# A planned graph-attention layer: scan sums reckoned later behind their loads, and new planner constants

## The chip, the core and the metric

The kernel runs on one core of a Trainium2 chip. The metric is the device time of one execution in microseconds (us). Five engines work side by side, each through a list of its own, in order: PE (matrix products; its weight loads are shown as PEld), DVE, ACT, POOL, and SP, which here only issues DMA transfers. An engine that waits at one instruction holds up all that stands behind it in its list.

## What is computed

One layer of a graph network: a layer norm and a ReLU of x (384 nodes, 1024 features), masked attention with 16 heads of 64, whose queries, keys and values each go through two linear layers, an output layer, and the residual. The mask comes from 6528 edges: an edge that is listed puts a positive weight in its cell, all other cells are minus infinity.

```python
h = relu(layernorm(x))
q = h @ wq.T + bq;  k = h @ wk.T + bk;  v = h @ wv.T + bv          # 1024 x 1024 each
q2 = heads(q @ wiq.T + biq);  k2 = heads(k @ wik.T + bik);  v2 = heads(v @ wiv.T + biv)
mask = full(-inf);  mask[src, dst] = softplus(edge_type_weights)[edge_type - 1]
scores = einsum('hnd,hmd->hnm', q2, k2) / 8 + mask
out = x + (softmax(scores) applied to v2, heads side by side) @ wo.T + bo
```

## The kernel before

**Products.** Each operand is kept as a high and a low plane, so that each product is three matmuls (`mm3`, L450 to L452: high by high, high by low, low by high). A weight matrix is cut in 8 chunks of 128 rows. The chunks run in the order v, q, iv, k (32 chunks), then iq and ik in turn (16), then o (8). For each chunk SP loads 512 KB into one of four raw buffers (`load`, L99), ACT makes the high plane (`split_hi`, L124 or L128), DVE the low plane (`split_lo`, L135 or L137), and PE multiplies. Results stay in PSUM banks: three of kind g, four of kind s, one of kind a; a product waits until its bank has been emptied. What empties a bank is `k_f` (L574, then L579 and L582 make the planes of k), `v2_hi` and `v2_lo` (L639, L643), `qk_hi` and `qk_lo` (L696, L702) and the like.

**Scans.** Scales for the planes of iv, k, iq, ik and o need sums over the weights before their products are reached. So 40 further loads, eight for each of these matrices, go through three buffers of a tile `scan` (`scan_load`, L144), and ACT sums each one (`scan_sum`, L149). A scan buffer is free again when its sum is done. PE adds the sums over rows (`bound_sums` L532, `row_sums` L537), and DVE turns them into scales (`g_scale` L553 to L561, `common_scale` L564 to L566). The high planes of the iq chunks wait for the scale of gq, those of ik for that of gk.

**Mask.** DVE finds double edges (L295, 51 steps), POOL scatters the weights into tables in DRAM (L306, 51 steps), and loads them back (`mask_load`, L314, three loads). DVE takes them over (`mask_select`, L318) and scales them (L569).

**Attention and output.** For each pair of heads p there are three row blocks. PE makes scores of two heads (`do_S`, L711) in two s banks, DVE adds the mask and takes the row minimum (`do_ttr`, L719), which empties the bank, ACT takes the exponential (L723), DVE the reciprocal (L726, L730). The weights are then made two planes, on one of two routes chosen by the table `pool`: on POOL (L733, ACT L738, POOL L744) or on DVE (ACT L740, DVE L746). SP transposes them by DMA (L751), PE multiplies with v2 (`do_av`, L760), ACT and DVE make two planes (L764, L767). The output is seven tiles (a block of 128 rows by 512 columns each; the last block's second half is cut in two of 256), each over the eight o chunks (`omm`, a call of `mm3` per chunk). PE goes through tiles and chunks in an order set by the planner, and starts while the last score steps still run. Four output tiles stand in s banks and three in g banks; the first use of a g bank for a tile waits for `qk_lo` of the last chunks, that of an s bank for `do_ttr` of the last scores. `finish` (L788) adds the residual and the tiles go out.

**The planner.** None of this order is written by hand. Each step is a task with its engine, an assumed duration and its dependencies. First a list of PE tasks is made: `at` holds a place for each (constants `pre`, `rate`, `ds`, `da`, `avlag`, `sp`, and `last` for the ends of the output tiles). Due times run backwards from it (`needed`), with shifts for some kinds (`due`). Then a greedy loop takes, again and again, the task that can start first by its reckoning, and among equals the one due first, and writes its instructions. The start is the latest of: the engine is free (`act0`, `dve0`, `pool0` at the beginning), each dependency has ended plus a margin, a buffer is free. The margin behind a task of SP is `late`; behind others `wait`, and for PE `slack`. `gate` holds SP back from issuing far ahead, `mll`, `selat` and `selby` set when the mask is reckoned to be there. So a constant moves no instruction's work; it moves places in the five lists.

Of the kernel before, what the change touches and what calls it, by code (L numbers as in the profile page):

```python
# [24 lines left out]

P = dict(
    pre=11.98,
    rate=2.66,
    avlag=7,
    slack=0.6,  # L30
    act0=6.72,
    dve0=4.77,
    pool0=8.64,
    pb=6,
    lead=3,
    first=[7],
    gate=3.2,
    mll=3.72,
    ds=[0.0, 0.0, 0.0, 0.0, 0.0, 0.0, 0.0, 0.47, 0.47, 0.47, 0.47, 1.09, 0.47, 1.58, 0.47, 0.47, 0.47, 1.04, 0.62,
        0.47, 0.23, 0.47, 0.47, 1.14],  # L40
    da=[1.19, 0.16, 1.23, 1.19, 1.19, -0.39, -0.39, -0.39],
    pool=[0, 1, 0, 1, 0, 1, 0, 1, 0, 1, 0, 1, 0, 1, 0, 1, 0, 1, 0, 1, 0, 1, 0, 1, 0, 0, 0, 1, 0, 1, 0, 1, 0, 1, 0,
        1, 0, 0, 0, 1, 0, 1, 0, 0, 0, 0, 0, 1],
    last=[5, 1, 2, 0, 3, 6, 4],
    sp=dict(row=5.6, bv=41.0, biv=55.0, turn=75.6, kb=88.0, v2t=111.14, gq=118.19, gk=126.86, ob=149.12),
    due=dict(v2l=-0.13, ss=0.11, gkd=-2.65, lo=1.37),
    wait=0.08,
    late=0.27,
    selat=3.85,
    selby=1.62,  # L50
)


# [1 line left out]
def gnn_kernel(ctx: ExitStack, tc: tile.TileContext, x, edges, erows, etw, wq, wk, wv, wiq, wik, wiv, wo,  # L55
# [14 lines left out]
    ACT, DVE, POOL, SP = nc.scalar, nc.vector, nc.gpsimd, nc.sync  # L70
# [595 lines left out]
    end = {("lo", 0): 0.0, ("lo", 1): 5.3, ("hi", 2): 3.1, ("hi", 1): 2.1, ("load", 4): 6.8, "keys": 7.2}  # L666
# [282 lines left out]
    for p in range(8):  # L949
# [7 lines left out]
        for j in range(3 * p, 3 * p + 3):  # L957
# [10 lines left out]
            for o in range(2):  # L968
                pool = (j, o) in ON_POOL
# [68 lines left out]
    due = {}  # L1038

    def needed(n):  # L1040
        if n not in due:
            eng, dur, _, _, lag = tasks[n]
            due[n] = 0.0
            far = n[0] == "sc"
            d = min([needed(u) - (4.6 if far and u != ("sc", n[1] + 1) else 0 if tasks[u][0] == eng else lag)
                     for u in users[n]], default=now) - dur
            k = "elo" if n[0] == "lo" and len(n) == 3 else n[0] if isinstance(n, tuple) else n
            due[n] = min(d, at.get(n, d)) + P["due"].get(k, 0.0)
        return due[n]
# [4 lines left out]
    def port(n, eng):  # L1054

        return eng == "POOL" and n[0] != "sc" or eng == "DVE" and n[0] in ("lo", "ms", "sel", "vlo", "Qlo", "kl", "det")
# [5 lines left out]
    while left:  # L1062
        best = None
        for n, (eng, dur, _, deps, lag) in left.items():
            if not all(d in end for d in deps):
                continue
            start = max([free[eng], free["port"] if port(n, eng) else 0.0])
            for d in deps:
                e = tasks.get(d, ("", 0, 0, 0, 0.0))
                start = max(start, end[d] + (0 if e[0] == eng else e[4] + (P["slack"] if eng == "PE" else P["late"] if e[0] == "SP" else P["wait"])))  # L1070
            if eng == "SP" and 0 < dur and n[0] != "turn":
                start = max(start, free["DMA"] - P["gate"])
            if n[0] == "sel":
                start = max(start, TB + P["selat"] + n[1] * P["selby"])
            ok = True
            for i, tag in enumerate(alloc[n]):
                w = len(ring[tag]) + alloc[n][:i].count(tag) - RING[tag]
                for f in ring[tag][w] if w >= 0 else []:
                    if f in end:
                        start = max(start, end[f] + (0 if tasks[f][0] == eng else tasks[f][4]))  # L1080
                    else:
                        ok = False
            if ok:
                rank = (start, -1.0 if n in FIRST else at[n] if eng == "PE" else needed(n))
                if best is None or rank < best[0]:
                    best = rank, n
        if best is None:
            raise ValueError(str([(n, [d for d in left[n][3] if d not in end], alloc[n]) for n in list(left)[:12]]))
        (start, _), n = best
        eng, dur, fn, _, lag = left.pop(n)  # L1090
        end[n] = free[eng] = start + dur
        if port(n, eng):
            free["port"] = end[n]
        if eng == "SP" and 0 < dur and n[0] != "turn":

            free["SP"] = start + 0.48
            end[n] = free["DMA"] = max(free["DMA"], start + 1.1) + dur
        if n[0] == "sc":
            end["sd", n[1]] = start + 5.6
        for i, tag in enumerate(alloc[n]):  # L1100
            ring[tag].append([frees[n][i]] if len(frees[n]) > i else [])
        fn()
# [39 lines left out]
```

## Time and profile before

| what | value |
|---|---|
| three runs | 275.53, 272.44, 274.82 us; median 274.82 |
| the profiled execution | 274.47 us |
| its span | 272.8 us, so 1.67 us around it |
| granted clock of PE | 0.999 |
| DMA | 72.44 MB, mean 266 GB/s |

The profile is of one execution. Busy time is counted per engine; a timeline row has the start in us from the span's start, the duration, and in brackets how long the engine stood idle before it and what ended that. Matmuls are pipelined, so a row's duration is longer than the distance from one start to the next; where rows are merged, "x4" gives their number. A row of the page's groups has the count, the busy time, the mean in ns, and the idle time before. Tile names are the program's, without buffer numbers: `whl` the weight planes, `raw` the loaded chunk, `scan` the scan buffer, `g`, `s`, `a` the banks (g also names some tiles in SBUF), `vhl` the planes of v2, `ma` the mask.

### The profile page before, as it was taken

To read this page: it belongs to the slowest core of one execution; us is meant where nothing else is said; L and a number is where in the kernel's file an instruction comes from. 1 tells how busy PE (TensorE), PEld (TensorE's weight loads), DVE (VectorE), ACT (ScalarE), POOL (GpSimd) and SP (SyncE) were. 2 spreads that over 40 slices of the span, in tenths; PEclk is the share of its full clock that TensorE was granted. 3 is DMA by queue.
4 is the path that set the end of the run, shared out by engine and by line. 5 is a ranking of instruction groups with operands and counts; after the bars stand their busy time and mean duration, and the time that the engine had idled before them with its cause. 6 is when DMAs were issued, how large, how long until landed. Compare 5 with 4: busy or idle time off the path is not lost. (4 is left out here: it accounts for less than half of the span.)

```text
span 272.8 us, 5010 instructions
## 1 busy us (share of the span) xinstructions
PE 264.7 (97%) x1636; PEld 188.3 (69%) x1636; DVE 215.4 (79%) x537; ACT 207.4 (76%) x394; POOL 134.7 (49%) x142
## 2 busy tenths in 40 slices
PE   7899999999999999999999999999999999999994
PEld 6899999999984444899996555555555554444552
DVE  3775578999995675658697999999899899989033
ACT  3886769879897997586978859998989898794100
POOL 5764685545475655466610005556771464335900
PEclk9999999999999999999999999999999999999999
DMA  6899998896999998989899974799999979956415
GB/s 236 267 307 416 369 406 321 221 412 248 353 340 367 382 407 285 320 286 322 268 345 404 356 274 154 118 198 203 231 202 160 248 153 171 324 114 117 87 46 187
DMA packets 58922, 72.44 MB, mean 266 GB/s; under 512 B 42640, under 2 KB 43280, under 8 KB 58896
## 3 DMA queue, kind: packets, MB, share of 16 engines
q1 hardware_dynamic: 56688, 70.26, 83.9%
q0 software_dynamic: 2064, 1.80, 2.3%
q8 instruction: 13, 0.21, 0.3%
q14 instruction: 13, 0.11, 0.1%
q10 hardware_dynamic: 144, 0.07, 0.1%
HBM read 59.27 MB, written 3.39 MB: 230 GB/s over the span
## 5 line engine op out<-in xcount | busy, mean ns | idle before, releaser
L452 PE MATMUL g<-g,whl 128*128 128x384 f32 (+1 forms) x304 | 100.7, 331 | 0.8 <-DVE whl L135 0.5
L450 PE MATMUL g<-g,whl 128*128 128x384 f32 (+1 forms) x304 | 101.3, 333 | 0.0
L451 PE MATMUL g<-g,whl 128*128 128x384 f32 (+1 forms) x304 | 100.6, 331 | 0.0
L306 POOL DMA_INDIRECT tab<-edge x51 | 58.9, 1154 | 40.6 <-DMA tab<-edge 27.2
L149 ACT ACTIVATE scan<-scan 128x1024 f32<-128x1024 f32 x40 | 42.1, 1052 | 16.0 <-DMA scan<-in_wik_dram 5.4
L733 POOL TENSOR_TENSOR e<-e,st 128x384 f32<-128x384 f32 x20 | 22.9, 1146 | 52.7 <-DVE st L726 28.4
L137 DVE TENSOR_TENSOR whl<-raw,whl 128x1024 fp32r<-128x1024 f32 x22 | 27.1, 1230 | 19.2 <-ACT whl L128 12.7
L452 PEld LDWEIGHTS g<-g,whl 128*128 128x128 f32 x176 | 33.0, 188 | 0.6 <-issue 0.6
L450 PEld LDWEIGHTS g<-g,whl 128*128 128x128 f32 x176 | 33.1, 188 | 0.3
L451 PEld LDWEIGHTS g<-g,whl 128*128 128x128 f32 x176 | 33.1, 188 | 0.0
L723 ACT ACTIVATE e<-e,st 128x384 f32<-128x384 f32 x48 | 28.9, 603 | 3.0 <-DVE st L719 3.0
L744 POOL TENSOR_TENSOR pp<-e,pp 128x384 f16<-128x384 f32 x20 | 22.1, 1110 | 15.2 <-ACT pp L738 15.1
L719 DVE CUSTOM_DVE_ANT_0 e<-s,ma,cols 128x384 f32<-128x384 f32 x48 | 27.3, 607 | 0.0
L128 ACT ACTIVATE whl<-raw 128x1024 fp32r<-128x1024 f32 x23 | 24.1, 1048 | 4.1 <-POOL edge L253 2.0
L135 DVE SCALAR_TENSOR_TENSOR whl<-raw,small,whl 128x1024 f16<-128x1024 f32 x16 | 21.0, 1321 | 4.7 <-ACT whl L124 4.7
L450 PE MATMUL s<-whl,g 128*128 128x512 f16 (+2 forms) x65 | 23.6, 363 | 0.5 <-DVE st L719 0.5
L451 PE MATMUL s<-whl,g 128*128 128x512 f16 (+2 forms) x65 | 23.6, 363 | 0.0
L452 PE MATMUL s<-whl,g 128*128 128x512 f16 (+2 forms) x65 | 23.5, 363 | 0.0
L124 ACT ACTIVATE whl<-raw,small 128x1024 f16<-128x1024 f32 x16 | 18.1, 1141 | 5.6 <-DMA raw<-in_wo_dram 4.4
L450 PEld LDWEIGHTS <-whl 128*128 128x128 f16 x128 | 12.5, 98 | 12.1 <-issue 4.9
L135 DVE SCALAR_TENSOR_TENSOR whl<-raw,cols,whl 128x1024 f16<-128x1024 f32 x16 | 20.6, 1294 | 0.0
L746 DVE SCALAR_TENSOR_TENSOR pp<-e,st,pp 128x384 f16<-128x384 f32 x28 | 20.0, 741 | 0.6 <-ACT pp L740 0.5
(184 smaller groups left out, 456.3 us busy)
## 6 DMA issues: line engine op xcount, KB each, us to landing
raw<-in_wv_dram SPq DMA_DIRECT2D x8, 512.0 KB
scan<-in_wiv_dram SPq DMA_DIRECT2D x8, 512.0 KB
raw<-in_wq_dram SPq DMA_DIRECT2D x8, 512.0 KB
scan<-in_wk_dram SPq DMA_DIRECT2D x8, 512.0 KB
raw<-in_wiv_dram SPq DMA_DIRECT2D x8, 512.0 KB
scan<-in_wiq_dram SPq DMA_DIRECT2D x8, 512.0 KB
raw<-in_wk_dram SPq DMA_DIRECT2D x8, 512.0 KB
scan<-in_wik_dram SPq DMA_DIRECT2D x8, 512.0 KB
```

The source lines that it names most:

```text
L128: nc.scalar.activation(hi, raw[w], AF.Copy)
L135: nc.vector.scalar_tensor_tensor(lo, raw[w], sc, hi, op0=OP.mult, op1=OP.subtract)
L137: (eng or nc.vector).tensor_tensor(lo, raw[w], hi.bitcast(F32), OP.subtract)
L149: ACT.activation(x, x, AF.Abs if n in ("iv", "o") else AF.Square, accum_out=l1[:, j, m:m + 1])
L306: nc.gpsimd.indirect_dma_start(out=tabs[c // RNG], out_offset=bass.IndirectOffsetOnAxis(ap=idx[:, c:c + 1], axis=0), in_=val[:, c:c + 1], ...
L450: nc.tensor.matmul(ps, lhi, rhi, start=first, stop=False)
L451: nc.tensor.matmul(ps, lhi, rlo, start=False, stop=False)
L452: nc.tensor.matmul(ps, llo, rhi, start=False, stop=last)
L719: DVE.tensor_tensor_reduce(es[j][o], sps[j][o][:, :N], ma[:, j % 3, :], nscale, 3.0e38, OP.add, OP.min, sts[j][:, o:o + 1])
L723: ACT.activation(es[j][o], es[j][o], AF.Exp, bias=sts[j][:, o:o + 1], scale=-1.0, accum_out=sts[j][:, 2 + o:3 + o])
L733: POOL.tensor_tensor(es[j][o], es[j][o], sts[j][:, 4 + o:5 + o].to_broadcast([128, N]), OP.mult)
L744: POOL.tensor_tensor(pls[j, o][:, 1, :], es[j][o], pls[j, o][:, 0, :], OP.subtract)
```

## The change

There is one new constant, `dl`. In the planner's loop the margin behind a task of SP becomes `late + dl` if the waiting task is a scan sum (`ss`), so these sums are reckoned ready 0.568 us later than anything else that waits for a load. `late` itself goes from 0.27 to 0.336. Other constants are set anew, and with them the lists of all engines come out in another order. The work itself is nearly the same: the table `pool` loses one entry, so that one half of one score step (step 16, second head) goes by DVE and ACT and no longer by POOL. `last` sets another order of the output tiles' last chunks, and with it which tile comes last and is cut in two pieces.

```diff
@@ -25,29 +25,30 @@
-    rate=2.66,
+    rate=2.666,
-    act0=6.72,
-    dve0=4.77,
-    pool0=8.64,
+    act0=6.868,
+    dve0=5.838,
+    pool0=8.736,
-    gate=3.2,
-    mll=3.72,
+    gate=3.239,
+    mll=3.154,
...
-    da=[1.19, 0.16, 1.23, 1.19, 1.19, -0.39, -0.39, -0.39],
+    da=[1.19, 0.16, 1.23, 1.48, -0.3, -0.37, -0.37, -0.37],
...
-    last=[5, 1, 2, 0, 3, 6, 4],
-    sp=dict(row=5.6, bv=41.0, biv=55.0, turn=75.6, kb=88.0, v2t=111.14, gq=118.19, gk=126.86, ob=149.12),
-    due=dict(v2l=-0.13, ss=0.11, gkd=-2.65, lo=1.37),
+    last=[5, 0, 2, 6, 3, 4, 1],
+    sp=dict(row=5.6, bv=41.0, biv=55.55, turn=75.6, kb=88.0, v2t=111.14, gq=118.19, gk=126.86, ob=147.73),
+    due=dict(v2l=1.03, ss=0.11, gkd=-2.65, lo=1.37),
     wait=0.08,
-    late=0.27,
-    selat=3.85,
-    selby=1.62,
+    late=0.336,
+    dl=0.568,
+    selat=3.916,
+    selby=1.857,
...
@@ -1067,7 +1068,7 @@
-                start = max(start, end[d] + (0 if e[0] == eng else e[4] + (P["slack"] if eng == "PE" else P["late"] if e[0] == "SP" else P["wait"])))
+                start = max(start, end[d] + (0 if e[0] == eng else e[4] + (P["slack"] if eng == "PE" else P["late"] + (P["dl"] if n[0] == "ss" else 0.0) if e[0] == "SP" else P["wait"])))
```

Left out are the row of `pool` and `ds`, a list that places the score steps two by two: steps 2 and 3 come 0.08 earlier in it, steps 20 to 23 by 0.82. The new line of `dl` moves all later line numbers by one, so that L149 of before is L150 of after, L702 is L703, and so on.

The first place is SP's list around the first scan loads of wo, at about 120 to 145 us. Before:

```order
L99 DMA raw<-in_wiq_dram 128x1024
L144 DMA scan<-in_wik_dram 128x1024
L99 DMA raw<-in_wik_dram 128x1024
L144 DMA scan<-in_wo_dram 128x1024
L99 DMA raw<-in_wiq_dram 128x1024
L144 DMA scan<-in_wo_dram 128x1024 x2
L99 DMA raw<-in_wik_dram 128x1024
L144 DMA scan<-in_wo_dram 128x1024 x3
```

The same stretch of SP's list after:

```order
L100 DMA raw<-in_wiq_dram 128x1024
L145 DMA scan<-in_wik_dram 128x1024
L145 DMA scan<-in_wo_dram 128x1024
L100 DMA raw<-in_wik_dram 128x1024
L145 DMA scan<-in_wo_dram 128x1024
L100 DMA raw<-in_wiq_dram 128x1024
L145 DMA scan<-in_wo_dram 128x1024
L100 DMA raw<-in_wik_dram 128x1024
L145 DMA scan<-in_wo_dram 128x1024 x3
```

The first wo scan load has moved ahead of a raw load of wik, and the second ahead of a raw load of wiq. ACT's list at the same time, before (the first L149 here is the last one of wik, the second the first of wo; `g_1435` holds the planes of k):

```order
L149 ACTIVATE scan,l_98<-scan 128x1024
L579 ACTIVATE g_1435<-f,cols 128x384
L149 ACTIVATE scan,l_98<-scan 128x1024
L128 ACTIVATE whl<-raw 128x1024
L639 ACTIVATE vhl<-s,small 128x8x64 x2
L579 ACTIVATE g_1435<-f,cols 128x384
L639 ACTIVATE vhl<-s,small 128x8x64
L149 ACTIVATE scan,l_98<-scan 128x1024
L639 ACTIVATE vhl<-s,small 128x8x64
L579 ACTIVATE g_1435<-f,cols 128x384
L639 ACTIVATE vhl<-a,small 128x8x64
L149 ACTIVATE scan,l_98<-scan 128x1024
```

And after:

```order
L580 ACTIVATE g_1435<-f,cols 128x384
L150 ACTIVATE scan,l_98<-scan 128x1024 x2
L129 ACTIVATE whl<-raw 128x1024
L640 ACTIVATE vhl<-s,small 128x8x64 x2
L580 ACTIVATE g_1435<-f,cols 128x384
L150 ACTIVATE scan,l_98<-scan 128x1024
L640 ACTIVATE vhl<-s,small 128x8x64 x2
L580 ACTIVATE g_1435<-f,cols 128x384
L150 ACTIVATE scan,l_98<-scan 128x1024
L640 ACTIVATE vhl<-a,small 128x8x64
```

An L579 has moved ahead of the last wik sum, and each of the next two wo sums ahead of one L639.

The second place is DVE's list in the tail, at about 229 to 234 us, where the last score steps and the first output products meet (`k_2881` before and `k_2854` after are the planes of the last k2). Before:

```order
L719 ISA e,st<-s,ma,cols 128x384
L719 ISA st 128x1
L135 SCALAR_TENSOR_TENSOR whl<-raw,small,whl 128x1024
L726 RECIPROCAL st<-st 128x2
L730 TENSOR_SCALAR st<-st 128x2
L726 RECIPROCAL st<-st 128x2
L730 TENSOR_SCALAR st<-st 128x2
L135 SCALAR_TENSOR_TENSOR whl<-raw,small,whl 128x1024
L702 SCALAR_TENSOR_TENSOR k_2881<-g,cols,k_2881 128x384
L746 SCALAR_TENSOR_TENSOR pp<-e,st,pp 128x384
L767 SCALAR_TENSOR_TENSOR g_1732<-a,small,g_1732 128x384
```

And after:

```order
L720 ISA e,st<-s,ma,cols 128x384
L720 ISA st 128x1
L703 SCALAR_TENSOR_TENSOR k_2854<-g,cols,k_2854 128x384
L136 SCALAR_TENSOR_TENSOR whl<-raw,small,whl 128x1024
L727 RECIPROCAL st<-st 128x2 x2
L731 TENSOR_SCALAR st<-st 128x2 x2
L136 SCALAR_TENSOR_TENSOR whl<-raw,small,whl 128x1024
L768 SCALAR_TENSOR_TENSOR g_1732<-a,small,g_1732 128x384
L747 SCALAR_TENSOR_TENSOR pp<-e,st,pp 128x384
```

The low plane of the last k2, which empties a g bank, has moved ahead of two low planes of wo and of the reciprocals. The third place is the end of the score steps on DVE, at about 241 to 247 us. Before:

```order
L719 ISA e,st<-s,ma,cols 128x384
L719 ISA st 128x1
L746 SCALAR_TENSOR_TENSOR pp<-e,st,pp 128x384
L767 SCALAR_TENSOR_TENSOR g_1732<-a,small,g_1732 128x384
L719 ISA e,st<-s,ma,cols 128x384
L719 ISA st 128x1
L726 RECIPROCAL st<-st 128x2 x2
L730 TENSOR_SCALAR st<-st 128x2
L135 SCALAR_TENSOR_TENSOR whl<-raw,small,whl 128x1024
L719 ISA e,st<-s,ma,cols 128x384
L719 ISA st 128x1
```

And after:

```order
L136 SCALAR_TENSOR_TENSOR whl<-raw,small,whl 128x1024
L727 RECIPROCAL st<-st 128x2
L731 TENSOR_SCALAR st<-st 128x2
L768 SCALAR_TENSOR_TENSOR g_1732<-a,small,g_1732 128x384
L747 SCALAR_TENSOR_TENSOR pp<-e,st,pp 128x384
L720 ISA e,st<-s,ma,cols 128x384
L720 ISA st 128x1
L720 ISA e,st<-s,ma,cols 128x384
L720 ISA st 128x1
L136 SCALAR_TENSOR_TENSOR whl<-raw,small,whl 128x1024 x2
```

The last two L719 now stand together, and two low planes of wo have moved behind them; before, one low plane stood ahead of the last L719.

More of the change, by code (lines that the diff above doesn't have):

```diff
@@ L36 @@
     first=[7],
-    gate=3.2,
-    mll=3.72,
-    ds=[0.0, 0.0, 0.0, 0.0, 0.0, 0.0, 0.0, 0.47, 0.47, 0.47, 0.47, 1.09, 0.47, 1.58, 0.47, 0.47, 0.47, 1.04, 0.62,
-        0.47, 0.23, 0.47, 0.47, 1.14],
-    da=[1.19, 0.16, 1.23, 1.19, 1.19, -0.39, -0.39, -0.39],
-    pool=[0, 1, 0, 1, 0, 1, 0, 1, 0, 1, 0, 1, 0, 1, 0, 1, 0, 1, 0, 1, 0, 1, 0, 1, 0, 0, 0, 1, 0, 1, 0, 1, 0, 1, 0,
+    gate=3.239,
+    mll=3.154,
+    ds=[0.0, -0.08, 0.0, 0.0, 0.0, 0.0, 0.0, 0.47, 0.47, 0.47, -0.35, 0.27, -0.35, 0.76, -0.35, -0.35, -0.35, -1.59,
+        -0.2, -0.35, -0.59, -0.35, -0.36, 0.31],
+    da=[1.19, 0.16, 1.23, 1.48, -0.3, -0.37, -0.37, -0.37],
+    pool=[0, 1, 0, 1, 0, 1, 0, 1, 0, 1, 0, 1, 0, 1, 0, 1, 0, 1, 0, 1, 0, 1, 0, 1, 0, 0, 0, 1, 0, 1, 0, 1, 0, 0, 0,
         1, 0, 0, 0, 1, 0, 1, 0, 0, 0, 0, 0, 1],
-    last=[5, 1, 2, 0, 3, 6, 4],
-    sp=dict(row=5.6, bv=41.0, biv=55.0, turn=75.6, kb=88.0, v2t=111.14, gq=118.19, gk=126.86, ob=149.12),
-    due=dict(v2l=-0.13, ss=0.11, gkd=-2.65, lo=1.37),
+    last=[5, 0, 2, 6, 3, 4, 1],
+    sp=dict(row=5.6, bv=41.0, biv=55.55, turn=75.6, kb=88.0, v2t=111.14, gq=118.19, gk=126.86, ob=147.73),
+    due=dict(v2l=1.03, ss=0.11, gkd=-2.65, lo=1.37),
     wait=0.08,
-    late=0.27,
-    selat=3.85,
-    selby=1.62,
+    late=0.336,
+    dl=0.568,
+    selat=3.916,
+    selby=1.857,
 )
```

## The prediction

> **What bounds the kernel now.** I read the page's busy line first, then the waits of PE, then busy time by stretch, and last the timelines around the places where PE stood.
>
> ```profile
> PE 264.7 (97%) x1636; PEld 188.3 (69%) x1636; DVE 215.4 (79%) x537; ACT 207.4 (76%) x394; POOL 134.7 (49%) x142
> ...
> PE g L452 <- DVE whl L135: 0.5, 1, 0.5
> ...
> PE g L452 <- issue: 0.3, 1, 0.3
> ...
> 222.00:258.00 36.00, 34.98 (x240) 17.95 (x240) 29.36 (x66) 24.32 (x55) 19.77 (x15) 1.00 0.80 163
> 134.00:158.00 24.00, 23.49 (x141) 17.77 (x140) 21.88 (x47) 19.07 (x30) 2.21 (x3) 1.00 1.00 364
> ```
>
> (In the stretches the columns are the length, then busy time of PE, PEld, DVE, ACT and POOL, the granted clock, the share of the DMA engines and GB/s.) PE is busy 97% of the span, at full granted clock in both stretches, and each of its own waits is under a microsecond or so. The change leaves PE's products as they are, so all that it can win is such holes. They lie in two stretches whose feeding work the change moves: 133 to 158 us, and the output products from 222 us. The others (start-up, and one at 42 us that the view calls "issue") keep their causes. A hole is best measured as the distance between two starts, less the usual pitch.
>
> ```profile
> 133.29 0.34 PE L452 MATMUL g<-g,whl 128*128 128x384 f32 x1
> 133.68 0.17 PE L537 MATMUL s<-l,small 128*128 128x9 bf16 x1
> ...
> 148.80 0.33 PE L450 MATMUL g<-g,whl 128*128 128x384 f16 x1
> 148.97 0.33 PE L451 MATMUL g<-g,whl 128*128 128x384 f16 x1
> 149.80 0.34 PE L452 MATMUL g<-g,whl 128*128 128x384 f16 x1 [0.51 <-DVE whl L135]
> ...
> 152.90 0.33 PE L450 MATMUL g<-g,whl 128*128 128x384 f16 x1
> 153.18 0.32 PE L451 MATMUL g<-g,whl 128*128 128x384 f16 x1
> ...
> 157.99 0.70 PE L711 MATMUL s<-k,q 64*128 64x384 f16 x4
> ...
> 225.81 0.49 PE L711 MATMUL s<-k,q 64*128 64x384 f16 x4
> ```
>
> The pitch is 0.17 us (148.80 to 148.97). So the holes are 0.22 (before 133.68), 0.66 (before 149.80), 0.11 (before 153.18), and 0.21 inside the four L711, which take 0.70 where four others take 0.49. Together **1.2 us**. The tail:
>
> ```profile
> 232.36 0.38 PE L451 MATMUL g<-whl,g 128*128 128x512 f16 x1
> 232.58 0.38 PE L452 MATMUL g<-whl,g 128*128 128x512 f16 x1
> 233.51 0.27 PE L450 MATMUL g<-whl,g 128*128 128x256 f16 x1 [0.56 <-DVE k L702]
> ...
> 245.84 0.38 PE L452 MATMUL s<-whl,g 128*128 128x512 f16 x1
> 246.68 0.27 PE L450 MATMUL s<-whl,g 128*128 128x256 f16 x1 [0.46 <-DVE st L719]
> ```
>
> Here the pitch is 0.22 and the two holes 0.71 and 0.62, together **1.3 us**. The 2.5 us of both stretches are 0.9% of 274.47: that is the most that the change can win by much.
>
> **The change, first place: the scan sums.** A scan sum (L149) stands in ACT's in-order list, and whatever stands behind it waits with it.
>
> ```profile
> 129.60 1.06 ACT L149 ACTIVATE scan<-scan 128x1024 f32<-128x1024 f32 x1 [2.25 <-DMA scan<-in_wo_dram]
> 142.65 1.06 ACT L149 ACTIVATE scan<-scan 128x1024 f32<-128x1024 f32 x1 [1.67 <-DMA scan<-in_wo_dram]
> 145.52 1.06 ACT L149 ACTIVATE scan<-scan 128x1024 f32<-128x1024 f32 x1 [1.21 <-DMA scan<-in_wo_dram]
> ...
> 122.84 0.60 ACT L579 ACTIVATE g<-f,cols 128x384 f16<-128x384 f32 x1
> ...
> 124.22 0.33 SPq L99 DMA_DIRECT2D raw<-in_wik_dram  x1
> 124.60 0.42 SPq L144 DMA_DIRECT2D scan<-in_wo_dram  x1
> ...
> 135.00 0.33 SPq L144 DMA_DIRECT2D scan<-in_wo_dram  x1
> ...
> 131.74 1.23 DVE L137 TENSOR_TENSOR whl<-raw,whl 128x1024 fp32r<-128x1024 f32 x1 [2.04 <-ACT whl L128]
> 132.88 1.40 DVE L643 SCALAR_TENSOR_TENSOR vhl<-s,small,vhl 128x512 f16<-128x512 f32 x2
> 144.34 0.62 DVE L582 SCALAR_TENSOR_TENSOR g<-f,cols,g 128x384 f16<-128x384 f32 x1 [1.54 <-ACT g L579]
> 147.05 1.53 DVE L318 COPY_PREDICATED ma<-mbs 128x1152 f32<-128x1152 int32 x1
> 148.47 1.27 DVE L135 SCALAR_TENSOR_TENSOR whl<-raw,cols,whl 128x1024 f16<-128x1024 f32 x1
> ...
> 142.66 0.18 PE L537 MATMUL s<-l,small 128*128 128x9 bf16 x1
> ```
>
> The reader should follow one thread. The first scan load of wo is issued at 124.60, directly behind a raw load that goes at 124.22, when its own buffer comes free. ACT stands 2.25 us for it until 129.60; DVE's L137 stands 2.04 us behind ACT; and the two L643 after it (132.88 and 1.40 long, the first done about 133.6) empty the bank that PE's L537 wants: the hole before 133.68. The late sums also empty their buffers late. The scan load of 135.00 waits for such a sum, ACT then stands 1.67 and 1.21 us more, L582 1.54 us, and the bound chain behind it brings L318 only at 147.05. From there DVE has no pause, and its L135 (148.47 and 1.27: 149.74) makes the largest hole; the next two come out of the same lateness.
>
> What the change does there, step by step. On SP, the scan load goes ahead of the raw load; a load holds SP for 0.4 us (124.22 to 124.60), which the raw load pays. The raw load's planes are those that PE wants at 149, so that is hidden. The scan load's buffer is the one emptied by the sum just ahead of the L128 and L579 of 122, so it can go at about 122.0: 2.6 us earlier (estimate). It took at most 5.0 us from issue to ACT's start (124.60 to 129.60); with half a microsecond for its neighbours it is there at 127.5. Then L149, L128, L639, L137 and L643 all come some 2 us earlier, and the first hole closes. On ACT, an L579 (0.6 us) moves ahead of the sum before this one, and the next sum moves ahead of one L639: that L639 waits 1.06 us more, inside the 2 us won. The buffers after it come free earlier too, so the load of 135.00 goes at about 132.4, and ACT's last two pauses shrink by about 2 us each. What is late next is the chain to L318, which needs PE's L537 of 142.66; its ten small DVE steps and L566 take 2.2 us (144.88 to 147.05, as the last L582 ends), so L318 begins near 145 and L135 ends near 147.8. PE wants it at 149.13 (148.97 and a pitch). All four holes close: **-1.2 us**. Bounds: if only the wait of 129.60 shrinks, -0.2; if the loads land no earlier at all, 0; better than -1.2 there is nothing.
>
> Has the DMA room for it? Three rows by stretch:
>
> ```profile
> 122.00:124.00 2.00, 2.00 (x14) 2.00 (x13) 1.03 (x1) 2.00 (x3) 0.96 (x1) 1.00 0.98 316
> 124.00:126.00 2.00, 2.00 (x13) 2.00 (x12) 1.73 (x4) 1.74 (x4) 1.15 (x1) 1.00 0.67 216
> 132.00:134.00 2.00, 1.95 (x13) 1.72 (x12) 2.00 (x3) 2.00 (x5) 1.95 (x2) 1.00 0.47 148
> ```
>
> From 122 to 124 the share is 0.98, so the early load first queues. Then it is 0.67, and 0.47 from 132 to 134, just where loads are held back by a buffer: an earlier issue finds room. Against it, the load of 135.00 took 7.6 us (to 142.65), for from 134 to 158 the share is 1.00.
>
> The Trainium skill (DMA: Bandwidth & Descriptors, section "Issuing engines are not separate DMA queues") says that transfers started by different engines run on the same 16 DMA engines and interleave. The 7.6 us, with POOL's mask loads started in that stretch, agree with it. By that rule alone an earlier scan load only pushes another back, and the first place would give 0.2 us at most, which is rival 2; the half-idle stretch before 134 is why I hold it less likely.
>
> **Second place: the tail.** DVE is 82% busy there (29.36 of 36.00), so each hole comes from what stands ahead in its list.
>
> ```profile
> 229.92 1.28 DVE L135 SCALAR_TENSOR_TENSOR whl<-raw,small,whl 128x1024 f16<-128x1024 f32 x1
> 232.85 0.61 DVE L702 SCALAR_TENSOR_TENSOR k<-g,cols,k 128x384 f16<-128x384 f32 x1
> 246.01 0.60 DVE L719 CUSTOM_DVE_ANT_0 e<-s,ma,cols 128x384 f32<-128x384 f32 x1
> ...
> L733 POOL TENSOR_TENSOR e<-e,st 128x384 f32<-128x384 f32 x20 | 22.9, 1146 | 52.7 <-DVE st L726 28.4
> L746 DVE SCALAR_TENSOR_TENSOR pp<-e,st,pp 128x384 f16<-128x384 f32 x28 | 20.0, 741 | 0.6 <-ACT pp L740 0.5
> ```
>
> The last L702, for whose bank PE waits until 233.51, now comes directly behind four L719, ahead of the L135 of 229.92, another L135 and four small steps. One half of a score unit also goes from POOL (L733, L744) to DVE (L746), upstream of this. POOL is at 49%, so what it saves, 1.15 us and another instruction, is worth nothing by itself; DVE pays 0.5 to 0.74. I take 0.6, as most of that time DVE is not idle. So L702 starts at 229.92 and 0.6, and ends near 231.1 instead of 233.46. PE now does an attention product earlier and some output tiles later, and asks for the bank near 230.8 (estimate: 233.51 less the hole, 0.71, and less some nine 512-wide matmuls of 0.22). So 0.3 of 0.71 stay: 0.4 won. The last L719 comes ahead of its L135 (1.28), so the 0.62 could go as well. What is moved back pays for it: the L135 behind L702 ends 0.6 to 1.1 us later than now, two or three more stand behind two further L719 (0.6 each), and on SP two raw loads of wo come behind more L751. I count the second hole as given back whole, to new waits of 0.2 to 0.3 each at two or three planes, and take **-0.4**. Bounds: -1.3 if nothing new waits; +2.4 if nothing is won and three planes are each 0.8 late. I stand nearer the first, since no L135 of the tail is among PE's waits now.
>
> **The rest.** Between 20 and 75 us some sums, row loads and bias steps change places, and near 165 us a bias sum comes earlier. PE's waits name none of these lines, so they count nothing; their cover is the planes' lead. If one lead goes, it costs one for one, and half a microsecond of that lies in the range.
>
> Sum: 274.47 - 1.2 - 0.4 = 272.87, so **272.9 us**. The profiled execution's 274.47 is the span of 272.8 and 1.67 around it; it stands 0.35 under the median of the runs, 274.82.
>
> **Rivals.**
> 1. Both places give all: 274.47 - 1.2 - 1.3 = 271.9 us. For it: each hole hangs on one short chain that the new lists shorten. Against it: DVE's 82% leave the moved planes little room.
> 2. The loads land no earlier, because DMA is full: 274.47 - 0.2 and 0 to 0.4 from the tail, about 274.1 us. For it the 7.6 us; against it the share of 0.47.
> 3. Slower: low planes of wo come late in the tail, behind the L719 and the later raw loads. If four of them each make PE wait 1.2 us, that is +4.8, with the first place's -1.2 some 278.1 us. It decides from the point where a plane is more than about a microsecond later than now plus its lead.
>
> **How the numbers follow.** Chances: forecast 0.54 (own range 272.1 to 273.7), rival 1 0.22, rival 2 0.12, rival 3 0.12. A measurement of this kernel tells about 1% from no change, so faster is below 272.07 and slower above 277.57. Rival 1 and a little of the forecast make faster 0.24; rival 3 makes slower 0.11; the same has 0.65. The range takes in rivals 1 and 2, a microsecond below rival 1 for the spread of the runs (272.44 to 275.53), and part of what late planes cost: 270.9 to 275.6.
>
> **What would show it.** Right: the first scan load of wo is issued near 122, no ACT wait at L149 over 1 us from 126 to 146, L318 begins near 145, PE waits for no L135 and no L702 from 133 to 158, and the tail's L702 ends before 231.5 with a hole of 0.3. Wrong: ACT still stands at the scans of wo, PE's products or pitch differ, or PE waits for L135 after 230 us.

## The result, and the profile after

The changed kernel takes 272.48 us (median of 20 runs, 271.04 to 273.91), the kernel before 274.39 (20 runs, 272.44 to 276.74). The medians differ by 1.9 us; the ratio of the runs is 0.9935, with a 95% interval of 0.9913 to 0.9957: 1.8 us less, 0.65%. The forecast was 272.9, 0.4 us above the median. The profiled execution took 272.39 us, with a span of 270.7 where the one of before had 272.8.

These are PE's own waits in the changed kernel, and its two stretches (columns as in the prediction):

```profile
PE g L373 <- DVE g L365: 0.4, 1, 0.4
PE s L712 <- DVE st L720: 0.3, 1, 0.3
PE s L451 <- DVE st L720: 0.3, 1, 0.3
PE g L453 <- DVE whl L138: 0.2, 1, 0.2
...
222.00:258.00 36.00, 35.32 (x240) 17.83 (x239) 28.42 (x59) 20.79 (x46) 17.36 (x13) 1.00 0.77 155
134.00:158.00 24.00, 24.00 (x150) 17.88 (x150) 22.37 (x44) 17.37 (x26) 2.23 (x3) 1.00 0.99 365
```

From 134 to 158 us PE is now busy for 24.00 of 24.00 us (23.49 before), and in the tail for 35.32 of 36.00 (34.98 before). The waits for L135 and for L702 of before are gone. Two new ones for L720 (L719 of before) stand in the tail. Here are SP, ACT and DVE in the first place after:

```profile
120.04 0.33 SPq L145 DMA_DIRECT2D scan<-in_wo_dram  x1
122.26 0.33 SPq L100 DMA_DIRECT2D raw<-in_wik_dram  x1
...
125.24 1.06 ACT L150 ACTIVATE scan<-scan 128x1024 f32<-128x1024 f32 x1 [0.80 <-DMA scan<-in_wik_dram]
126.53 1.06 ACT L150 ACTIVATE scan<-scan 128x1024 f32<-128x1024 f32 x1
138.26 1.04 ACT L150 ACTIVATE scan<-scan 128x1024 f32<-128x1024 f32 x1
141.03 1.04 ACT L150 ACTIVATE scan<-scan 128x1024 f32<-128x1024 f32 x1
...
144.20 1.53 DVE L319 COPY_PREDICATED ma<-mbs 128x1152 f32<-128x1152 int32 x1
145.62 1.26 DVE L136 SCALAR_TENSOR_TENSOR whl<-raw,cols,whl 128x1024 f16<-128x1024 f32 x1
```

The scan load goes at 120.04, 2.2 us ahead of the raw load. ACT has the three wo sums that had waited, the first, fifth and sixth, at 126.53, 138.26 and 141.03, where they stood at 129.60, 142.65 and 145.52, and the waits of 2.25, 1.67 and 1.21 us in front of them are gone. The last wik sum, at 125.24, now waits 0.80. L319 begins 2.85 us earlier. And the tail after, on PE, DVE, ACT and SP:

```profile
228.93 0.28 PE L451 MATMUL g<-whl,g 128*128 128x256 f16 x1
236.95 0.33 PE L712 MATMUL s<-k,q 64*128 64x384 f16 x1
237.63 0.64 PE L712 MATMUL s<-k,q 64*128 64x384 f16 x5 [0.35 <-DVE st L720]
241.67 0.27 PE L453 MATMUL g<-whl,g 128*128 128x256 f16 x1
242.28 0.38 PE L451 MATMUL s<-whl,g 128*128 128x512 f16 x1 [0.33 <-DVE st L720]
...
226.42 0.61 DVE L703 SCALAR_TENSOR_TENSOR k<-g,cols,k 128x384 f16<-128x384 f32 x1
236.63 0.17 DVE L727 RECIPROCAL st<-st 128x2 f32<-128x2 f32 x1 [2.18 <-ACT e L724]
236.95 0.62 DVE L720 CUSTOM_DVE_ANT_0 e<-s,ma,cols 128x384 f32<-128x384 f32 x1
...
234.25 1.15 ACT L125 ACTIVATE whl<-raw,small 128x1024 f16<-128x1024 f32 x1 [2.68 <-DMA raw<-in_wo_dram]
...
215.47 14.01 SPq L752 DMA_TRANSPOSE pt<-pp  x8
229.54 1.04 SPq L100 DMA_DIRECT2D raw<-in_wo_dram  x2
```

L703 ends at 227.03, and PE uses the bank at 228.93 with no wait: the hole of 0.71 is gone whole. In place of the other one there are two. One matmul of the last score step starts at 236.95, and the next only at 237.63 (usual distance 0.08: a hole of 0.60); then 241.67 to 242.28 is 0.50 too long. The chain behind them reads from the last row up: eight transposes hold SP until 229.5, the raw load of wo comes late, ACT stands 2.68 us at L125, the exponentials stand behind it, DVE's L727 stands 2.18 us behind those, and L720 behind that empties the bank.

### The profile page after: what moved, and what is told of

It is laid out like the page before. It is cut to its first block, busy times and chain, and to the rows that moved or that the text cites. A ratio compares the mean times of both kernels' runs of the same rounds, so it can differ in the third digit from the quotient of the medians.

```text
span 270.7 us, 5004 instructions
## 1 busy us (share of the span) xinstructions
PE 264.2 (98%) x1636; PEld 188.3 (70%) x1636; DVE 218.6 (81%) x538; ACT 207.5 (77%) x394; POOL 131.1 (48%) x140
## 5 line engine op out<-in xcount | busy, mean ns | idle before, releaser
L307 POOL DMA_INDIRECT tab<-edge x51 | 57.2, 1121 | 43.3 <-DMA tab<-edge 32.7
L734 POOL TENSOR_TENSOR e<-e,st 128x384 f32<-128x384 f32 x19 | 20.6, 1084 | 54.7 <-DVE st L727 30.1
L150 ACT ACTIVATE scan<-scan 128x1024 f32<-128x1024 f32 x40 | 42.0, 1049 | 6.4 <-DMA scan<-in_wik_dram 4.7
L720 DVE CUSTOM_DVE_ANT_0 e<-s,ma,cols 128x384 f32<-128x384 f32 x48 | 27.2, 610 | 1.1 <-PE s L712 1.1
L745 POOL TENSOR_TENSOR pp<-e,pp 128x384 f16<-128x384 f32 x19 | 20.2, 1069 | 14.7 <-ACT pp L739 14.5
L125 ACT ACTIVATE whl<-raw,small 128x1024 f16<-128x1024 f32 x16 | 18.1, 1141 | 7.5 <-DMA raw<-in_wo_dram 4.8
L747 DVE SCALAR_TENSOR_TENSOR pp<-e,st,pp 128x384 f16<-128x384 f32 x29 | 21.8, 783 | 0.0
```

The source lines that it names most:

```text
L150: ACT.activation(x, x, AF.Abs if n in ("iv", "o") else AF.Square, accum_out=l1[:, j, m:m + 1])
L307: nc.gpsimd.indirect_dma_start(out=tabs[c // RNG], out_offset=bass.IndirectOffsetOnAxis(ap=idx[:, c:c + 1], axis=0), in_=val[:, c:c + 1], ...
L720: DVE.tensor_tensor_reduce(es[j][o], sps[j][o][:, :N], ma[:, j % 3, :], nscale, 3.0e38, OP.add, OP.min, sts[j][:, o:o + 1])
L734: POOL.tensor_tensor(es[j][o], es[j][o], sts[j][:, 4 + o:5 + o].to_broadcast([128, N]), OP.mult)
L747: DVE.scalar_tensor_tensor(pls[j, o][:, 1, :], es[j][o], sts[j][:, 4 + o:5 + o], pls[j, o][:, 0, :], op0=OP.mult, op1=OP.subtract)
```

## The experiments

**How they are read.** The times of single runs spread by 1% and more, so beside the ratios I use PE's own list as a clock. In it, the same in every kernel up to a few rows, four points are fixed: matmul 84 (about 15 us, the start-up is over), 601 (in the first k chunk), 867 (the last product ahead of the first score), and 1301 (behind scores 16 and 17, shortly before the tail). The table gives the distance between their starts in each profile, in us. "Old" and "new" say whose lists the first place and the tail have. The end is that of PE's last matmul.

| kernel | first place | tail | 84 to 601 | 601 to 867 | 867 to 1301 | 84 to 1301 | 1301 to end |
|---|---|---|---|---|---|---|---|
| before | old | old | 95.93 | 46.25 | 60.27 | 202.45 | 51.05 |
| c1, before again | old | old | 95.88 | 46.29 | 60.61 | 202.78 | 52.33 |
| e7 | old | old | 96.97 | 45.22 | 60.02 | 202.21 | 51.91 |
| e9 | old | new | 96.13 | 45.22 | 61.27 | 202.62 | 50.76 |
| e2 | old | new | 96.94 | 45.22 | 60.02 | 202.18 | 50.22 |
| e1 | new | old | 97.08 | 45.22 | 60.96 | 203.26 | 51.17 |
| e3 | new on SP | old | 95.38 | 45.22 | 60.02 | 200.62 | 51.01 |
| e4 | new on ACT, DVE | old | 95.33 | 45.22 | 60.02 | 200.57 | 49.92 |
| after | new | new | 95.82 | 45.22 | 60.02 | 201.06 | 50.82 |
| c2, after again | new | new | 96.57 | 45.22 | 60.02 | 201.81 | 50.79 |
| e8 | new | new | 95.34 | 45.22 | 60.02 | 200.58 | 50.36 |
| e5 | new | new, loads back | 95.92 | 45.22 | 60.02 | 201.16 | 49.67 |
| e6 | new | new, loads back | 95.31 | 45.22 | 60.02 | 200.55 | 49.96 |
| e10, e6 again | new | new, loads back | 97.34 | 45.22 | 60.02 | 202.58 | 49.67 |

In edits of lists the tasks have the planner's names: `load` a raw load and `sl` a scan load by number, `ss` a scan sum, `hi` and `lo` the planes of a chunk, `ke` and `kl` the planes of k, `kf` and `vf` what comes before them, `v2h` and `v2l` the planes of v2, `turn` a transpose. Where lists are edited they are written out in the kernel, so its line numbers are higher by about 108.

**The kernel before again (c1).** No edit but the lists written out.

> The kernel before once more (its lists written out, the same instructions on every engine). Ratio 1.000 within the noise. It shows whether the holes belong to the lists or to one execution. Theory A (they belong to the lists): holes of about 1.2 us again between 133 and 158 us, and 1.3 us in the tail after 230. Theory B (in the first place the lists only fail when a transfer happens to land late): the first place has no hole in this execution or quite another sum, the tail still has 1 us or more.

Ratio 0.9993 (0.9952 to 1.0034). Its holes, on PE:

```profile
132.98 0.34 PE L560 MATMUL g<-g,whl 128*128 128x384 f32 x1
134.22 0.17 PE L645 MATMUL s<-l,small 128*128 128x9 bf16 x1 [0.90 <-DVE vhl L751]
...
PE s L558 <- DVE st L827: 1.1, 2, 0.6
PE g L558 <- DVE k L810: 1.0, 1, 1.0
...
222.00:258.00 36.00, 33.87 (x228) 17.10 (x226) 30.11 (x70) 25.09 (x57) 18.65 (x15) 1.00 0.80 164
```

The first place loses almost the same again (46.29), but at another spot: one hole of 1.07 at the row sum, where the first profile had 0.22 there and most of it at L135. The tail is worse than in the first profile, 33.87 busy of 36.00, and its hole behind the last k2 is 1.19 instead of 0.71. So the size of a single hole is of one execution, and neither theory A nor B holds as written.

**The changed kernel again (c2).** No edit but the lists written out.

> The changed kernel once more (its lists written out, the same instructions on every engine). Ratio to before 0.9935 (0.990 to 0.997). Both theories: no hole from 133 to 158 us; after 230 us again about 1.1 us, near S23 (ACT stands at the high plane of the wo chunk loaded late) and before the second s bank.

Ratio 0.9916 (0.9886 to 0.9946). No hole in the first place, 0.62 and 0.50 in the tail, the same two places. As expected.

**The margin alone (e1).**

```diff
-    late=0.27,
+    late=0.27, dl=0.568,
...
-... P["late"] if e[0] == "SP" else ...
+... P["late"] + (P["dl"] if n[0] == "ss" else 0.0) if e[0] == "SP" else ...
```

> The kernel before with the new margin (late + dl for scan sums, dl 0.568) and no other constant changed. Its PE list is that of before, so the tail is unchanged. Theory (the scan loads and sums are the first place, worth 1.2 to 1.3 us): the four PE holes between 133 and 158 us go, those before 233.5 and 246.7 us stay at 0.7 and 0.6; 273.1 us where before gives 274.39, ratio 0.9953 (0.993 to 0.997). Rival (the gain of the whole change came from the other constants): ratio 0.999 to 1.001 and the holes stay. Rival 2 (all of the 1.9 us comes from dl): ratio 0.9935.

This alone gives, in the first place, the lists of the changed kernel in all but one detail (a v2 high plane ahead of a chunk's), and leaves PE's list and the tail untouched; it also moves scan sums, bias steps and steps of the mask between 30 and 107 us. Ratio 0.9967 (0.9939 to 0.9995). No hole stands from 133 to 158 us, as forecast, but the execution that was profiled is a late one (275.58 where the median is 274.41): it lost 1.5 us at 42 us, and 0.9 at the second pair of scores. That wait and its cause on ACT:

```profile
167.00 0.50 PE L711 MATMUL s<-k,q 64*128 64x384 f16 x4 [0.66 <-DVE k L702]
...
157.89 1.15 ACT L124 ACTIVATE whl<-raw,cols 128x1024 f16<-128x1024 f32 x1 [3.43 <-DMA raw<-in_wik_dram]
...
140.26 0.78 POOL L314 DMA_DIRECT2D mbs<-tab  x1 [1.94 <-DMA tab<-edge]
141.31 0.75 POOL L314 DMA_DIRECT2D mbs<-tab  x1 [0.27 <-DMA tab<-edge]
```

In this execution the scatter ended late, POOL issued the second and the third mask load at 140.26 and 141.31 (the third went at 137.36 in the profile of before), and a raw load issued after them held ACT for 3.43 us. That the margin alone closes the first place's holes is not shown by this profile: PE came to the first place late (97.08), and e2 and e7, whose lists there are old, have no hole either after 96.94 and 96.97. What speaks for the margin are the lists, and a ratio that lies just clear of 1.

**The margin set to zero in the changed kernel (e2).**

```diff
-    dl=0.568,
+    dl=0.0,
```

> The changed kernel with dl set to 0, all other new constants kept. Theory: the four holes between 133 and 158 us come back, the tail stays as in the changed kernel (one hole less at 233 us, two new ones near 237 and 242 us), so only the tail's gain is left: -0.4 us against before, ratio 0.9985 (0.996 to 1.000). Rival (the other constants carry the gain): ratio 0.9935. Rival 2 (all from dl): 1.000.

Ratio 0.9925 (0.9889 to 0.9960), against my 0.9985: a miss, and the value of the first rival, that the other constants carry the gain. It has the first place's lists of before, and no hole there; of the tail's two holes only the second is there, 0.50 at 243.57. Its ACT and SP:

```profile
122.97 0.33 SPq L100 DMA_DIRECT2D raw<-in_wik_dram  x1
123.35 0.42 SPq L145 DMA_DIRECT2D scan<-in_wo_dram  x1
...
127.78 1.06 ACT L150 ACTIVATE scan<-scan 128x1024 f32<-128x1024 f32 x1 [0.40 <-DMA scan<-in_wo_dram]
```

The raw load, and the scan load behind it, went 1.25 us earlier than in the profile of before, and ACT's wait shrank from 2.25 to 0.40. But the table shows where that gain was spent: PE had lost 1 us more at 42 us than in the profile of before (96.94), and the sum from 84 to 1301 is 202.18, no better than the other kernels with these lists. The profiled execution (273.82) is 0.95 slower than this kernel's median, and why the median is so good stays open. So the times do not show that the changed kernel needs the margin: without it, it is as fast. What the margin is worth rests on the table.

**Only SP's two swaps in the kernel before (e3).**

```diff
 sl.31
+sl.32
 load.33
-sl.32
+sl.33
 load.34
-sl.33
 sl.34
```

> The kernel before with its own lists, except that on SP the first two wo scan loads stand ahead of the raw load behind which each stood. Theory (the load that SP held back is the head of the thread): the load is issued near 122 us, ACT's wait of 2.25 us for it is gone, all four holes go or nearly so: -1.0 us, ratio 0.9964 (0.995 to 0.998). Rival (the sums stand too early in ACT's list; the loads land no earlier): -0.2 us or nothing, ratio 0.999 to 1.000.

Ratio 0.9944 (0.9908 to 0.9980), all four holes gone. SP and ACT:

```profile
119.20 0.33 SPq L252 DMA_DIRECT2D scan<-in_wo_dram  x1
121.41 0.33 SPq L207 DMA_DIRECT2D raw<-in_wik_dram  x1
...
125.08 1.06 ACT L257 ACTIVATE scan<-scan 128x1024 f32<-128x1024 f32 x1 [1.17 <-DMA scan<-in_wik_dram]
126.65 1.05 ACT L257 ACTIVATE scan<-scan 128x1024 f32<-128x1024 f32 x1
```

The load goes at 119.2, and ACT waits for nothing at 126.65; the sum ahead, the last of wik, waits 1.17. The rival, that loads land no earlier, is out. And here PE came early (95.38) and lost nothing behind: its 200.62 from matmul 84 to 1301 lies below every sum with the old lists (202.18 to 202.78).

**Only ACT's and DVE's lists (e4).**

```diff
 hi.30
+ke.2
 ss.31
-ke.2
 ss.32
...
 ke.3
+ss.33
 v2h.2
-ss.33
 v2h.3
 ke.4
+ss.34
 v2h.4
-ss.34
```

(On ACT also `v2h.5` ahead of `hi.32` and `ss.35` ahead of `ke.5`; on DVE `v2l.4` ahead of `kf.5`, `v2l.5` ahead of `kl.5`, `lo.37` ahead of the first mask scale.)

> The kernel before with its own lists, except that ACT's and DVE's lists between 118 and 158 us have the new order (one k plane ahead of a sum, each of the next sums ahead of a v2 plane, two v2 low planes and one low plane earlier on DVE); SP as before. Theory (SP's order is the head): ACT still stands about 2.2 us at the first wo sum, the hole before 133.7 us stays, the later ones shrink a little since the following scan load goes 0.6 us earlier: -0.2 us, ratio 0.999 (0.997 to 1.001). Rival (ACT's order carries it): ratio 0.9955 and four holes gone.

Ratio 0.9987 (0.9950 to 1.0025), as forecast, but the profile speaks for the rival: no hole, 45.22. SP and ACT:

```profile
122.03 0.33 SPq L207 DMA_DIRECT2D raw<-in_wik_dram  x1
122.41 0.42 SPq L252 DMA_DIRECT2D scan<-in_wo_dram  x1
...
127.00 1.06 ACT L257 ACTIVATE scan<-scan 128x1024 f32<-128x1024 f32 x1 [1.62 <-DMA scan<-in_wo_dram]
```

ACT still stands 1.62 us at the first wo sum, as the theory has it, yet nothing on PE comes of it. The profiled execution took 271.47, the lowest of all its runs (median 275.50), so it shows what is possible and not what is usual; its twelve runs reach from there to 279.41. Between SP's order and ACT's the ratios speak for SP's, but their intervals overlap.

**The two raw loads put back (e5).** In the changed kernel's SP list:

```diff
 turn.15.1
+load.52
 turn.16.0
 turn.16.1
+load.53
 turn.17.0
 turn.17.1
-load.52
-load.53
 turn.18.0
```

> The changed kernel, with two raw loads of wo (chunks 52 and 53) put back ahead of four and two of the transposes that SP has ahead of them since the change. Theory (the tail's new holes come from these late loads: ACT stands 2.7 us at the high plane, the exponentials stand behind it, DVE 2.2 us behind those): both new holes, 0.60 and 0.50, go: -1.0 us against the changed kernel, ratio to before 0.990. Rival (DVE is full there, and the hole only moves): 0.9935, holes of 1 us elsewhere in the tail.

Both holes go. SP, ACT, DVE and the stretch:

```profile
224.50 0.53 SPq L209 DMA_DIRECT2D raw<-in_wo_dram  x1
...
232.16 1.13 ACT L234 ACTIVATE whl<-raw,small 128x1024 f16<-128x1024 f32 x1
...
235.05 0.16 DVE L836 RECIPROCAL st<-st 128x2 f32<-128x2 f32 x1
...
222.00:258.00 36.00, 36.00 (x250) 18.34 (x247) 29.18 (x60) 21.58 (x48) 17.36 (x14) 1.00 0.84 158
```

The load goes at 224.50 and not at 229.54, ACT's L234 waits for nothing, nor does DVE's reciprocal, and PE is busy for 36.00 of 36.00 us. The chain of the tail is shown. (e6 and e10 below, with the same edit, have neither hole; e2 and e8, without it, have only the second, so the first one does not come in every execution.) In time it is 0.9917 (0.9876 to 0.9957) beside c2's 0.9916 on the same chip, where I forecast 1.0 us less: in the profiles the tail is 1.1 us shorter (50.79 and 49.67), but the intervals reach 0.8 to 1.1 us to each side, and the times don't show it.

**Chunk 7 ahead as well (e6, and e10 again; e8 without the loads; e7 in the kernel before).** All four have

```diff
 ss.1
+hi.7
 va.4
-hi.7
...
 det.12
+lo.7
 vf.4
 vf.5
-lo.7
```

on ACT and DVE (e6 and e10 with the edit of e5 too, e8 on the changed kernel, e7 on the kernel before).

> As e5, and besides the planes of chunk 7 (high on ACT, low on DVE) stand ahead of the fifth v eviction, for the hole at 42 us (0.6, 0.5, 1.4, 1.5, 0 and 0 us in six profiles). Theory (a hole before the mask is ready is worth its full size): 0.6 us less in the mean than e5, ratio 0.988. Rival (what is won before 110 us is absorbed by later waits for loads): as e5, with a hole at 120 to 158 us.

> The kernel before with its own lists, except that the planes of chunk 7 (high on ACT, low on DVE) stand ahead of the fifth v eviction. Theory (the first place is held to an absolute time by loads and sums, not by PE: what PE wins earlier it loses there): the hole at 42 us is 0, PE comes to 110 us 0.5 to 1.4 us earlier than in the kernel before, and the holes from 133 to 158 us grow by as much; the first score product stays at 157.3 to 158.0 us, ratio 1.000 (0.997 to 1.003). Rival (each hole is worth its size): the first score product at 156.9 us, ratio 0.998.

> The changed kernel with the same move of chunk 7. Theory: the first place has room since the change, so that the win at 42 us lasts: first score product at 156.0 us (156.1 and 157.3 in two profiles of the changed kernel), holes of the tail as in the changed kernel (1.1 us); 0.8 us less than the changed kernel in the mean, ratio to before 0.990. Rival (absorbed later): 0.9925.

> The kernel of e6 once more: the changed kernel, the two raw loads put back, chunk 7 ahead. Theory: no hole over 0.35 us behind the start; PE's end at 266 us, ratio to before 0.989 (0.986 to 0.992), that is 0.4% under the changed kernel. Rival (one lucky execution): a ratio of 0.9925 and holes at 42 us or in the tail.

Ratios: e6 0.9898 (0.9848 to 0.9948), e8 0.9901 (0.9867 to 0.9934), e10 0.9894 (0.9864 to 0.9925), e7 0.9981 (0.9950 to 1.0011). The first three are close to their forecasts, but their intervals hold their rivals' ratios too. In e8 the first score product starts at 155.92 (forecast 156.0); the tail's holes are other ones than forecast: 0.32 before 241.40, and 0.39 at 228.92, where PE waits for the bank that the last k2's low plane empties. In e6 that wait is 0.31. The hole at 42 us is 0 in e6 and e8, but 1.05 us in e7 and 1.92 in e10:

```profile
40.78 0.34 PE L562 MATMUL g<-g,whl 128*128 128x384 f32 x1
42.87 0.41 PE L560 MATMUL g<-g,whl 128*128 128x384 f32 x1 [1.75 <-DVE f L589]
...
41.03 1.23 DVE L247 TENSOR_TENSOR whl<-raw,whl 128x1024 fp32r<-128x1024 f32 x1 [1.46 <-ACT whl L238]
42.18 1.01 DVE L589 TENSOR_TENSOR f<-g,rrow 128x384 f32<-128x384 f32 x2
```

In e10 the raw chunk was late, DVE stood 1.46 us at the low plane, and the eviction that I had put behind it came late: PE now waits for its bank and not for the plane. My edit moved the hole. So e10's forecast, no hole over 0.35 and PE's end at 266, failed (it ended at 267.4). Half of the edit, ACT's alone, may be better; it wasn't tried. And e7 could not show what it was made for, since the hole that it was to close stayed open. It fits the same theory in the other direction: it lost 1.05 us at 42 us and 0.46 at 90.6, and had no hole from 105 to 222 us.

**The tail alone (e9).** The kernel before, with the changed kernel's lists, `pool` and `last` from about 215 us on (PE, ACT, DVE, POOL and SP). The edit on SP, with `last` and one entry of `pool` (POOL's `nrm.16.1` goes to DVE):

```diff
-    last=[5, 1, 2, 0, 3, 6, 4],
+    last=[5, 0, 2, 6, 3, 4, 1],
...
 turn.15.1
-load.52
 turn.16.0
+turn.16.1
 turn.17.0
-load.53
-turn.16.1
 turn.17.1
-load.54
-load.55
+load.52
+load.53
 turn.18.0
```

> The kernel before with the lists of the changed kernel from about 215 us on (the tail, with the pair moved from POOL to DVE and the new order of the last output chunks). Theory: the first place as in the kernel before (first score product at 157.5 to 158 us), the tail from there to PE's end 110.2 to 110.9 us where the kernel before took 111.3 and 113.0: 0.5 to 2 us less, ratio 0.996 (0.993 to 0.998). Rival (the tail's gain needs the first place): ratio 1.000.

Ratio 0.9981 (0.9957 to 1.0004). The tail is 50.76, with the same two holes as in the changed kernel (0.53 and 0.50), so it needs nothing of the first place. But at the second pair of scores this execution lost 1.25 us (61.27 where 60.02 is usual), so that from the first score product to PE's end it took 111.8 us, outside my 110.2 to 110.9. It lost them as e1 did: POOL's last two mask loads went late (139.84 and 140.62), and ACT stood 3.49 us at the same raw load. The first place lost nothing here (45.22), against the theory. In time it is not told from no change.

**The best of them.** e10, the changed kernel with the two loads back and chunk 7 ahead, has 0.9894 (0.9864 to 0.9925), and 0.9898 in its first run. It beats the kernel before. That it beats the changed kernel too (0.9935 and 0.9916) is likely by the tails of the profiles, and not settled by the times; nor is it settled that the loads add anything, since e8, without them, has 0.9901.

## Why the prediction was right, step by step

**What bounds the kernel: right.** In twelve of fourteen profiles the stretch from matmul 601 to 867 takes 45.22 us, in ten that from 867 to 1301 takes 60.02, to a hundredth: PE's pitch is the same in all. What differs between the kernels up to there, and between two executions of one, is holes.

**First place, 1.2 us: right in the mean, and right in its steps for the pair of profiles that it was read from and checked on.** The scan load went at 120.0 (forecast 122), L318 began at 144.2 (145), no scan sum from 126 to 146 us waited over 1 us, and all four holes went; the stretch fell from 46.25 to 45.22, and the next, which has the fourth hole, from 60.27 to 60.02. Over all profiles the way from matmul 84 to 1301 takes 202.2 to 202.8 us with the old lists (five profiles, mean 202.45), and 201.35 in the mean of the nine with new lists there: 1.1 us, though the nine reach from 200.55 to 203.26 and three of them have chunk 7 moved as well. By the times alone it stays open, since e2 is as fast without the new lists there. What I had wrong is what the holes are. I priced them as if they belonged to the lists. With the old lists, the sum hardly moves whether PE loses 0.5 or 1.5 us at 42 us: PE runs into loads and sums that come at a time of their own, and a loss ahead of that costs nothing. With the new lists that time lies earlier, PE isn't held, and the early hole counts in full: eight of nine sums are the first column plus 105.24. That reading comes from the table; no experiment that sets the early hole at will stands behind it. For the old lists it rests on four profiles: before and c1 lost 0.6 and 0.5 us at 42 us and 1.3 and 1.7 behind matmul 601, e7 and e2 lost 1.5 and 1.6 ahead of it and nothing behind. e9 and e1 lost theirs at the second pair of scores, with old lists and with new ones.

**The head of the thread: half right.** I named the load that SP held back. SP's swap alone frees the first place (e3); in the one profile of it, so do ACT's and DVE's lists alone (e4, 200.57). In these two profiles either end of the chain gives the microsecond of room.

**Tail, 0.4 us: the sum fits, in part by luck; one step failed.** The tail lost 0.39 us of holes in the first pair of profiles (1.49 before, with one of 0.15 before 241.85 that I had left out; 1.10 after). Its length fell by 0.23: without their holes the two tails take 49.56 and 49.72, so PE's new order itself costs 0.16. Over all profiles it is 51.23 in six with old lists (49.92 to 52.33) and 50.59 in five with new ones (50.22 to 50.82): 0.64. "0.3 of 0.71 stay" was too careful for the profile after: none stayed. But that hole is of one execution too: 0 to 1.19 in the six profiles with old lists, and 0.39 and 0.31 in e8 and e6 with the new one. "The second hole given back to late low planes" failed: no low plane was late. The new holes came from the raw load behind the transposes, which I had named, but through ACT: a high plane that waits for a load holds the exponentials, and those hold DVE's next row minimum. e5 shows it, and that 0.8 us (50.59 to 49.77 in the mean of three profiles) lay in that step alone. So two errors of about 0.3 us met: more was won at the first hole than I took, and the new holes cost more (1.10) than the 0.77 that went with the other two.

**The moved pair and the rest: nothing seen, as forecast.** POOL's busy time fell from 134.7 to 131.1 us and DVE's rose from 215.4 to 218.6; no wait of PE names either. No run changed the pair by itself. For one execution the half microsecond that I left for the rest was too small: the hole at 42 us, whose causes I took as kept, was 0 to 1.9 us.

**The sum.** 1.1 and 0.64 make 1.74 by the table; the times say 1.8, with an interval of 1.2 to 2.4; the forecast was 1.6. With the spread of the first term, they agree more closely than the profiles can promise.

**The rivals.** Rival 2, that earlier loads only push others back, fell: the load issued 4.6 us earlier (120.04 for 124.60) was there for a sum 3.1 us earlier, and the first place was worth 1.1 and not 0.2. The rule of the Trainium skill behind it (DMA: Bandwidth & Descriptors, "Issuing engines are not separate DMA queues") agrees with the 3.43 us that ACT waited for a raw load behind POOL's late mask loads in e1. It didn't decide here: the DMA engines had room, and their share from 124 to 126 us rose from 0.67 to 0.90. Rival 3, late low planes, did not happen. Rival 1, all holes of both places gone, is what e5's profile came to, with a list that the planner did not find.

## What to carry to other kernels

Read the holes from a second profile before you price them one by one: with the old lists the sum over 200 us moved by 0.6 us in five profiles, while a single hole went from 0 to 1.1 us, and with the new lists even the sum moved by 2.7. Ask of each hole whether something behind it comes at a fixed time, since then what is won ahead of it may be lost again. And when a load is moved behind other issues of its queue, follow what stands behind its first user on that user's engine; the wait turned up two engines further on.

## What had not been expected

Two executions of one kernel differ by more than this change is worth, and where it was traced it came from when transfers land: the hole at 42 us was 0 to 1.9 us over fourteen profiles, and POOL issued its last mask load at 137.36 in the profile of before and at 141.31 in e1. Between such events PE keeps time to 0.01 us over 60 us.
